# Two banks in turn for the sums of y and for delta, and a convolution in six steps whose relu term TensorE adds in the bank

## The chip, the cores and the metric

The kernel runs on one core of a Trainium2 chip. The metric is the time of one execution on the device, in microseconds. TensorE (PE) does the matmuls, VectorE (DVE) and GpSimd (POOL) the elementwise work, ScalarE (ACT) the activations and copies, and SyncE (SP) issues the DMAs. Each engine works through its own queue in order and waits at an instruction until what it needs is there. A matmul writes to a bank of PSUM, of 512 fp32 numbers for each of 128 partitions.

## The reference

The model has an input of 4 images of 64 x 64 positions with 96 channels and two layers. The first is a convolution and a selective scan over 192 inner channels with 16 states each, in four directions; the second is attention with a feed-forward part. What matters here is in the first:

```python
def selective_scan(u, delta, A, Bs, Cs, D, delta_bias):
    ...
    delta = jax.nn.softplus(delta + delta_bias[None, :, :, None])
    def step(h, inp):
        ut, dt, Bt, Ct = inp
        dA = jnp.exp(dt[..., None] * A[None])
        h = dA * h + (dt * ut)[..., None] * Bt[:, :, None, :]
        y = jnp.einsum('bkdn,bkn->bkd', h, Ct)
        return (h, y)
...
xz = bilinear(x, W_in, s_in, b_in)
xp, z = jnp.split(xz, 2, axis=-1)
xc = xp.transpose(0, 3, 1, 2)
t = bq_quad(xc + move0_b[None, :, None, None])
...
t = jax.lax.conv_general_dilated(t, Wb, (1, 1), [(1, 1), (1, 1)], dimension_numbers=('NCHW', 'OIHW', 'NCHW'))
t = t + conv_b[None, :, None, None]
t = t + rp_b0[None, :, None, None]
t = jnp.where(t >= 0, t, prelu_a[None, :, None, None] * t)
t = t + rp_b1[None, :, None, None] + xc
xconv = jax.nn.silu(t)
...
out_y = selective_scan(xs, dts, A, Bs, Cs, Ds.reshape(K, Dn), dt_bias.reshape(K, Dn))
```

The prelu is a*t + (1 - a)*relu(t). The convolution's inputs and weights are signs, so the kernel holds them in fp8. `_gn(x)`, the group norm ahead of the layer, subtracts for each three channels their mean over an image, for which the kernel first forms sums over channels.

## The kernel before

**Pieces.** The scan is cut into 1536 pieces: 4 images x 4 directions (the order is in `KORD`) x 4 chunks of 1024 positions x 6 groups g of 32 channels x 4 quarters q of 4 states. A piece is a tile of 128 rows (32 channels x 4 states) by 1024 positions. `Scans.run` (L1323) goes through them one after the other. In step i it issues, in this order:

- loads for later pieces (`dl`: delta and delta times u; `bc`: B and C);
- the earlier directions' sums, once in four pieces (`load_sums`), and the copy of the last column of piece i-1's state for the next chunk (`carry`, ACT, L1271);
- if i mod 8 is 3: `evacuate(i - 4)`, in which ACT copies the sums of y out of PSUM (L1316) and four stores are noted;
- `decay(i + 1)`: ACT takes the exponential into a PSUM tile dA (L1231; there are two of these);
- `reduce(i - 3)`: PE sums over states with four matmuls (L1302) into the bank of y, and adds the earlier directions' sums at the end of a group (L1307). One bank holds two groups, that is eight pieces;
- `inject(i + 4)`: POOL multiplies delta times u by B, into a tile w (nine of these in turn, free again after `reduce`);
- a product h x C left to POOL by the step before, if any;
- `scan(i)`: DVE's scan, and then the product h x C on DVE, or left to POOL for the next step. Which one is decided when the program is built, from a tally of both engines' work (L1248 to L1258).

All DVE and POOL work beside the scan goes through one helper and has its line, L401. Stores are noted in `Later` and issued on SP at the end of that or a later step (L420).

**Lanes.** Beside the pieces, two kinds of generators are advanced by one stage in each step. Their stages lie between `yield`s. If i mod 8 is 0, a new `prepare` (L1130) is begun: it forms delta for a part of a chunk. Its stages are: eight matmuls into the bank dps (L1167); Abs and Relu on ACT (L1172, L1173); Exp and Ln, the latter into the bank (L1175, L1176); PE adds the relu part in the bank with an identity matmul (L1179); DVE multiplies by u (L1181); ACT copies delta out (L1185), and a store (`dld`) is noted, from which `dl` is loaded later. Three such prepares run ahead of the first piece. The other is the back lane, one generator after the other for the images: the prologue of image b + 2 (convolution among it) and the epilogue of image b (normalisation, attention, feed-forward).

**The convolution** (L567 to L635). An image has 16 parts: two halves of the channels by eight strips of 512 positions. A part has 18 taps, fp8 matmuls into one bank (L577), in four stages of 5, 4, 5 and 4, and a fifth stage in which ACT forms v and r = relu and PE forms xc in a second bank, pz. In the first four stages of the next part the part is finished: stage 0, two DVE additions into pz (L585 and L586: pz = S*pz + v, then pz = pz + (1 - a) r, `oma`); stage 1, Sign and Exp on ACT (L590, L598); stage 2, Ln and Exp (L600, L601); stage 3, u = pz * e on DVE (L604) and the copy of u by columns into `ut` (ACT, L614; POOL, L612, for image 0, whose prologue runs alone). Four parts fill one `ut`, which is then stored to `utd`; the rest of the prologue (`rw`) reads it to form the other directions, with `xr` on ACT (L659).

**csum** (L508 to L516): 32 matmuls with x as the weights and a column of ones, all added in one bank, then a copy (`cs`) and a matmul over groups of channels.

**PSUM.** dA takes two tiles of two banks. The other four banks are b0 and b1 for the back lane, y, and dps.

Of the kernel before, what the change touches and what calls it, by code (L numbers as in the profile page):

```python
# [53 lines left out]
def hybrid_kernel(ctx: ExitStack, tc: tile.TileContext, a: dict, out: bass.AP):  # L54
# [82 lines left out]
    acs, acb, oma = ctile("acs", [96, 2]), ctile("acb", [96, 2]), ctile("oma", [96, 2])  # L137

# [18 lines left out]
    def weights():  # L157
# [28 lines left out]
        def transposed(dst, srcs):  # L186

            count[0] += 1
            ps = p.ps.tile([128, 1024], BF16, name=f"tps{count[0]}", tag=("y", "dps")[count[0] % 2])
# [87 lines left out]
        nc.vector.tensor_scalar(oma, pv[:, :, PRELU], -1.0, 1.0, ALU.mult, ALU.add)  # L277
        yield
# [72 lines left out]
        ps = p.ps.tile([128, 512], F32, name="tpd", tag="dps")  # L351
# [125 lines left out]
def prologue(c, b, xts=None):  # L477
# [11 lines left out]
    with tc.tile_pool(name=f"xg_{b}", bufs=1) as xgp:  # L489
# [3 lines left out]
        with tc.tile_pool(name=f"cv_{b}", bufs=1) as cvp:  # L493
# [14 lines left out]
            csum = bank("csum", 0)[0:96, 0:1]  # L508
            for i in range(NT):
                nc.tensor.matmul(csum, xts[i // 8][:, i % 8, :], c.ones1, start=(i == 0), stop=(i == NT - 1))  # L510
                if i % 8 == 7:
                    yield
            cs = f32("cs")[0:96, 0:1]
            nc.scalar.copy(cs, csum)
            gsum = bank("gsum", 1)[0:96, 0:1]
# [48 lines left out]
            prev = None  # L564
            two = c.p.dA.tile([128, CH], F32, name=f"cv2_{b}", tag="dA") if alone else None
            utp = sub.enter_context(tc.tile_pool(name=f"ut_{b}", bufs=1))
            for n, part in enumerate(parts + [None]):  # L567
# [5 lines left out]
                for s in range(4):  # L573
                    if part:
                        for j, t in taps[(0, 5, 9, 14)[s] : (5, 9, 14, 18)[s]]:
# [5 lines left out]
                            )  # L581
                    if prev:
                        ph, pq, pz, v, r, pn = prev
                        if s == 0:
                            c.vec.scalar_tensor_tensor(pz, pz, pv[:, ph, S_X : S_X + 1], v, ALU.mult, ALU.add)  # L585
                            c.vec.scalar_tensor_tensor(pz, r, c.oma[:, one(ph)], pz, ALU.mult, ALU.add)  # L586
                        elif s == 1:

                            sg = f32("sg" + pn)[0:96, 0:128]
                            nc.scalar.activation(  # L590
                                sg.bitcast(F8).rearrange("p (h e i) -> p h e i", h=8, e=2),
                                pz.rearrange("p (h i e) -> p h e i", h=8, e=2), AF.Sign, saturate=False,
                            )
                            for m in range(3):
                                g0 = 64 * (m // 2) + 32 * ph
                                c.later.store(xgw[g0 : g0 + 32, m % 2, 128 * pq : 128 * pq + 128], sg[m::3, :])
                            e = f32("e" + pn)[0:96]
                            nc.scalar.activation(e, pz, AF.Exp, scale=-1.0)  # L598
                        elif s == 2:
                            nc.scalar.activation(e, e, AF.Ln, bias=1.0)  # L600
                            nc.scalar.activation(e, e, AF.Exp, scale=-1.0)  # L601
                        else:
# [3 lines left out]

                            if pq % 4 == 0:
                                ut = utp.tile([96, IW, 32], F32, name=f"ut{pn}_{b}", tag="ut")
                            at = 8 * (pq % 4)
                            dst, src = ut[:, :, at : at + 8], u.rearrange("p (h w) -> p w h", w=IW)  # L610
                            if alone:
                                nc.gpsimd.tensor_copy(dst, src)  # L612
                            else:
                                nc.scalar.copy(dst, src)  # L614
                            if pq % 4 == 3:
                                rows = slice(8 * pq - 24, 8 * pq + 8)
                                c.later.store(
                                    c.utd[b][ph].rearrange("p (w h) -> p w h", h=IH)[:, :, rows], ut, after=1
                                )
                    yield  # L620
                if part:
# [9 lines left out]
                    )  # L631
                    prev = (h, q, pz, v, r, nm)
                    yield
            c.later.flush()
            sub.close()  # L635


# [459 lines left out]
class Scans:  # L1097
# [225 lines left out]
    def run(self, back):  # L1323
# [20 lines left out]
        for m in (1, 2):  # L1344
            self.load_dl(m)
# [113 lines left out]
```

## Time and profile before

| what | value |
|---|---|
| median of 3 runs (lowest to highest) | 5541.44 us (5539.87 to 5541.87) |
| the profiled execution | 5540.64 us |
| its span, first to last instruction | 5538.9 us |
| mean granted clock of TensorE | 0.714 |
| first scan to end of the last scan | 269.0 to 5421.4 us |

The page gives the span in 40 equal slices of 138 us. Each digit is the busy share of a slice in tenths, and PEclk is the granted clock of TensorE, in tenths:

```profile
PE   6456665576557766577656766544676564444677
...
DVE  3299999999999999899999999999999999999984
ACT  4467776777666667677766666755556775555554
POOL 2199999999999999899999999999999999999981
PEclk8667776678767876667777777766787766566778
```

After two slices of prologue and before the last, DVE and POOL are busy for 90% or more almost throughout, while PE and ACT go up and down with the stage of the back lane. By the number of the piece, the back lane has the convolution of image 1 from 69 to 149, that of image 2 from 264 to 344 and that of image 3 from 647 to 727; epilogues and the other prologue stages fill most of the rest, and for 264 pieces (1000 to 1093, 1290 to 1355, 1372 to 1475) it waits, with nothing to do beside the scan.

### The profile page before, as it was taken

Reading aid. Unit: us, or ns where it says so; the run is one execution under the profiler, and the core shown is the slowest. Engines: PE = TensorE matmul, PEld = TensorE weight load, DVE = VectorE, ACT = ScalarE, POOL = GpSimd, SP = SyncE. Lnnn points to the kernel's source line nnn. Section 1 sums busy time; section 2 is a strip of 40 time slices with the busy share of each in tenths; the row PEclk is TensorE's granted clock in tenths of the full one; section 3 lists DMA queues with packets and bytes.
Section 4 is the critical chain, followed back from the end, with each engine's and each line's share of the span. In section 5 each row is a group of like instructions: output and inputs, shape, how many; then the busy total and the mean of one; then the engine's idle time right before and its main releaser. Section 6 shows DMA issues by size and latency. Waiting matters only on the chain. (4 is left out here: it accounts for less than half of the span.)

```text
span 5538.9 us, 62371 instructions
## 1 busy us (share of the span) xinstructions
PE 3432.7 (62%) x20197; PEld 1356.7 (24%) x20197; DVE 5052.4 (91%) x3237; ACT 3556.7 (64%) x5564; POOL 4994.2 (90%) x2262
## 2 busy tenths in 40 slices
PE   6456665576557766577656766544676564444677
PEld 3222222222223222222222222211232121111223
DVE  3299999999999999899999999999999999999984
ACT  4467776777666667677766666755556775555554
POOL 2199999999999999899999999999999999999981
PEclk8667776678767876667777777766787766566778
DMA  4456666866766566666656566665666665665652
GB/s 78 118 179 198 207 194 193 258 193 199 220 203 194 194 205 199 218 217 207 205 193 212 185 200 210 212 211 191 210 215 186 191 205 198 205 208 190 207 159 60
DMA packets 613244, 1069.93 MB, mean 193 GB/s; under 512 B 225083, under 2 KB 343924, under 8 KB 611124
## 3 DMA queue, kind: packets, MB, share of 16 engines
q1 hardware_dynamic: 599428, 1065.88, 61.4%
q8 instruction: 159, 2.61, 0.2%
q10 hardware_dynamic: 13488, 0.07, 0.1%
q14 instruction: 169, 1.38, 0.1%
HBM read 833.20 MB, written 229.38 MB: 192 GB/s over the span
## 5 line engine op out<-in xcount | busy, mean ns | idle before, releaser
L401 POOL TENSOR_TENSOR w<-dl,bc 128x1024 f32<-128x1024 f32 x1536 | 3579.9, 2356 | 166.7 <-PE yp L1302 93.2
L1231 ACT ACTIVATE dA<-dl,anm 128x1024 f32<-128x1024 f32 x1536 | 1715.6, 1117 | 477.0 <-DVE w L401 291.5
L1302 PE MATMUL yp<-w,sum 128*32 128x256 f32 x12288 | 1261.6, 507 | 1083.2 <-ACT ys L1316 621.9
L401 DVE TENSOR_TENSOR_SCAN dA<-dA,cy,w 128x1024 f32<-128x1024 f32 x706 | 1654.4, 2343 | 94.7 <-ACT dA L1231 83.4
L401 POOL TENSOR_TENSOR w<-h,bc 128x1024 f32<-128x1024 f32 x596 | 1402.6, 2353 | 93.7 <-DVE h L401 85.2
L401 DVE TENSOR_TENSOR w<-dA,bc 128x1024 f32<-128x1024 f32 x940 | 1151.4, 1225 | 47.7 <-DVE dA L401 0.5
L401 DVE TENSOR_TENSOR_SCAN h<-dA,cy,w 128x1024 f32<-128x1024 f32 x446 | 1043.3, 2340 | 9.2 <-ACT dA L1231 8.7
L1302 PEld LDWEIGHTS yp<-w,sum 128*32 128x32 f32 x12288 | 308.0, 127 | 2136.9 <-issue 705.4
L1271 ACT COPY cy<-dA 128x1 f32<-128x1 f32 x707 | 110.8, 157 | 692.0 <-DVE w L401 690.7
L401 DVE TENSOR_TENSOR_SCAN dA<-dA,w 128x1024 f32<-128x1024 f32 x234 | 534.2, 2283 | 22.3 <-ACT dA L1231 18.0
L577 PE MATMUL cv<-tp,cw 96*96 96x512 fp8e5 x1152 | 359.9, 456 | 85.6 <-ACT r L627 70.5
L401 DVE TENSOR_TENSOR_SCAN h<-dA,w 128x1024 f32<-128x1024 f32 x150 | 341.8, 2279 | 24.4 <-POOL w L401 23.6
L1179 PE MATMUL dps<-sp,ident 128*128 128x512 f32 x378 | 356.8, 1043 | 0.0
L1307 PE MATMUL yp<-ya,back 128*128 128x256 f32 x576 | 237.8, 534 | 0.0
L577 PEld LDWEIGHTS <-cw 96*96 96x96 fp8e5 x1152 | 159.0, 146 | 277.5 <-issue 223.8
L1271 ACT COPY cy<-h 128x1 f32<-128x1 f32 x445 | 82.7, 186 | 145.6 <-DVE h L401 144.5
L847 PE MATMUL yc<-eys,mean 96*96 96x512 f32 x240 | 134.6, 713 | 33.3 <-DMA eys<-yd 14.5
L1307 PEld LDWEIGHTS yp<-ya,back 128*128 128x128 f32 x576 | 123.9, 248 | 127.8 <-issue 97.1
L1172 ACT ACTIVATE pd<-dps,dbias,pvd 128x512 f32<-128x512 f32 x189 | 143.8, 761 | 16.4 <-PE dps L1167 13.0
L1173 ACT ACTIVATE sp<-dps,dbias,pvd 128x512 f32<-128x512 f32 x189 | 144.7, 766 | 0.0
L401 DVE TENSOR_TENSOR pd<-dps,pu 128x512 f32<-128x512 f32 x189 | 127.6, 675 | 4.6 <-DMA dl<-dld 4.3
L1316 ACT COPY ys<-yp 128x512 f32<-128x512 f32 x192 | 111.7, 582 | 30.2 <-PE yp L1307 24.3
(282 smaller groups left out, 4017.6 us busy)
## 6 DMA issues: line engine op xcount, KB each, us to landing
dl<-dld SPq DMA_DIRECT2D x768, 512.0 KB
bc<-bcd SPq DMA_DIRECT2D x512, 512.0 KB
dld<-pd SPq DMA_DIRECT2D x126, 512.0 KB
yd<-ys SPq DMA_DIRECT2D x768, 64.0 KB
dld<-pd SPq DMA_DIRECT2D x126, 256.0 KB
ya<-yd SPq DMA_DIRECT2D x192, 128.0 KB
pu<-ud SPq DMA_DIRECT2D x32, 512.0 KB
pu<-utd SPq DMA_DIRECT2D x31, 512.0 KB
```

The source lines that it names most:

```text
L401: return getattr(self.eng, name)(out, *args, **kw)
L577: nc.tensor.matmul(ps, c.cw[:, j, t, 96 * h : 96 * h + 96], tpad[j][:, 8 * q + dy : 8 * q + dy + 8, dx : dx + IW], start=(j == 0 and t == ...
L847: self.c.nc.tensor.matmul(ps, w, x, start=(i == 0), stop=(i == len(pairs) - 1))
L1172: nc.scalar.activation(d[:, 0], ps, AF.Abs, scale=sc, bias=bi)
L1173: nc.scalar.activation(t, ps, AF.Relu, scale=sc, bias=bi)
L1179: nc.tensor.matmul(ps, c.ident, t, start=False, stop=True, skip_group_check=True)
L1231: c.nc.scalar.activation(t, self.dlt[i // NQ][0], AF.Exp, scale=c.anm[:, g, NQ * KORD[e] + q : NQ * KORD[e] + q + 1])
L1271: self.c.nc.scalar.copy(self.carries[g, q], h[:, CH - 1 : CH])
L1302: c.nc.tensor.matmul(y[32 * x : 32 * x + 32, g % 2, :], c.sum4, prod[:, 256 * x : 256 * x + 256], start=(q == 0), stop=(q == NQ - 1 and no ...
L1307: c.nc.tensor.matmul(y[:, g % 2, :], w, src, start=False, stop=(n == len(more) - 1))
L1316: c.nc.scalar.copy(t, y[:, :, ::-1] if k >= 2 else y)
```

## The change

Six edits, which go through the same functions:

1. **Banks.** The separate bank dps is gone. The sums of y alternate between two banks, y0 and y1, by eights of pieces. A prepare forms delta in the one that the sums do not use at that moment (`bank()`). Two set-up transposes take y0 and y1 as well.
2. **Order.** `evacuate` is issued after `decay(i + 1)`, no longer ahead of it.
3. **Prepares.** They begin at i mod 8 = 3, and have one more `yield` between Ln and the identity matmul. A fourth one runs ahead of the first piece, after the first three loads of `dl`; for that one more tile of the pool w is used at the start.
4. **Convolution** of images 1 to 3. Taps come four to a stage, in five stages, and with that of v and r there are six. The second addition on DVE is replaced by a matmul into pz with a diagonal matrix of 1 - a (`omad`, made once by two POOL instructions), in a stage of its own; Sign and Exp, Ln and Exp, and u follow one stage later each. The copy by columns is put off to stage 0 of the part that follows, and for the last part to just ahead of the final flush of stores.
5. **csum.** Eight matmuls with the ones as weights give a row of 4 x 96 sums; ACT copies the row, and four small matmuls turn and add it into a column, with one more `yield`.
6. **Carries.** One tile of four columns per group for four tiles of one column.

```diff
@@ prologue, csum
-            csum = bank("csum", 0)[0:96, 0:1]
-            for i in range(NT):
-                nc.tensor.matmul(csum, xts[i // 8][:, i % 8, :], c.ones1, start=(i == 0), stop=(i == NT - 1))
-                if i % 8 == 7:
+            csum = bank("csum", 0)[0:1, 0 : 4 * DM]
+            for i in range(0, NT, 4):
+                nc.tensor.matmul(
+                    csum, c.ones1, xts[i // 8][:, i % 8 : i % 8 + 4, :].rearrange("p i e -> p (i e)"),
+                    start=(i == 0), stop=(i == NT - 4),
+                )
+                if i % 8 == 4:
                     yield
+            row = f32("csr")[0:1, 0 : 4 * DM]
+            nc.scalar.copy(row, csum)
+            ps = bank("cst", 1)[0:96, 0:1]
+            for i in range(4):
+                nc.tensor.matmul(
+                    ps, row[:, DM * i : DM * i + DM], c.ones1[0:1, :], start=(i == 0), stop=(i == 3)
+                )
+            yield
             cs = f32("cs")[0:96, 0:1]
-            nc.scalar.copy(cs, csum)
-            gsum = bank("gsum", 1)[0:96, 0:1]
+            nc.scalar.copy(cs, ps)
+            gsum = bank("gsum", 0)[0:96, 0:1]
@@ prologue, convolution
-                for s in range(4):
+                for s in range(4 if alone else 5):
                     if part:
-                        for j, t in taps[(0, 5, 9, 14)[s] : (5, 9, 14, 18)[s]]:
+                        per = 5 if alone else 4
+                        for j, t in taps[per * s : min(18, per * s + per)]:
...
+                    if s == 0 and turned:
+                        by_columns(*turned)
+                        turned = None
                     if prev:
                         ph, pq, pz, v, r, pn = prev
                         if s == 0:
                             c.vec.scalar_tensor_tensor(pz, pz, pv[:, ph, S_X : S_X + 1], v, ALU.mult, ALU.add)
-                            c.vec.scalar_tensor_tensor(pz, r, c.oma[:, one(ph)], pz, ALU.mult, ALU.add)
+                            if alone:
+                                c.vec.scalar_tensor_tensor(pz, r, c.oma[:, one(ph)], pz, ALU.mult, ALU.add)
+                        elif s == 1 and not alone:
+                            nc.tensor.matmul(pz, c.omad[:, ph], r, start=False, stop=True, skip_group_check=True)
...
+            if turned:
+                by_columns(*turned)
             c.later.flush()
@@ Scans
+    def bank(self):
+        return max(0, self.at - 3) // 8 % 2
@@ prepare
-        ps = spare[3] if spare else p.ps.tile([128, 512], F32, name=f"dps_{nm}", tag="dps")
+        ps = spare[3] if spare else p.ps.tile([128, 512], F32, name=f"dps_{nm}", tag=f"y{1 - self.bank()}")
...
         nc.scalar.activation(ps, d[:, 0], AF.Ln, bias=1.0)
+        yield
         yield
@@ scan
-            self.carries[g, q] = c.p.cy.tile([128, 1], F32, name=f"cy_{i}", tag=f"cy{g}{q}")
+            if q == 0:
+                self.cys[g] = c.p.cy.tile([128, NQ], F32, name=f"cy_{i}", tag=f"cy{g}")
+            self.carries[g, q] = self.cys[g][:, q : q + 1]
@@ reduce
-            self.ydone[i // 8] = c.p.ps.tile([128, 2, 256], F32, name=f"yp_{i}", tag="y")
+            self.ydone[i // 8] = c.p.ps.tile([128, 2, 256], F32, name=f"yp_{i}", tag=f"y{i // 8 % 2}")
@@ run
-        w = [c.p.w.tile([128, CH], F32, name=f"w_s{x}", tag="w") for x in range(7)]
+        w = [c.p.w.tile([128, CH], F32, name=f"w_s{x}", tag="w") for x in range(8)]
...
+        u = c.p.pu.tile([128, CH], F32, name="pu_s", tag="pu")
+        for _ in self.prepare((w[7].rearrange("p (t l) -> p t l", t=2), w[4][:, 512:CH], u, ps[1][:, 512:CH])):
+            pass
...
+            if i + 1 < n:
+                self.decay(i + 1)
             if i % 8 == 3 and i > 8:
                 self.evacuate(i - 4)
-            if i + 1 < n:
-                self.decay(i + 1)
...
-            if i % 8 == 0 and self.todo:
+            if i % 8 == 3 and self.todo:
```

## The prediction

> **What bounds the kernel now.** I read the shares of busy time first, then the groups of instructions, then the waits, and at last busy time by stretches, since shares are means over stages.
>
> ```profile
> PE 3432.7 (62%) x20197; PEld 1356.7 (24%) x20197; DVE 5052.4 (91%) x3237; ACT 3556.7 (64%) x5564; POOL 4994.2 (90%) x2262
> ...
> L401 POOL TENSOR_TENSOR w<-dl,bc 128x1024 f32<-128x1024 f32 x1536 | 3579.9, 2356 | 166.7 <-PE yp L1302 93.2
> ...
> L1302 PE MATMUL yp<-w,sum 128*32 128x256 f32 x12288 | 1261.6, 507 | 1083.2 <-ACT ys L1316 621.9
> ...
> L401 POOL TENSOR_TENSOR w<-h,bc 128x1024 f32<-128x1024 f32 x596 | 1402.6, 2353 | 93.7 <-DVE h L401 85.2
> L401 DVE TENSOR_TENSOR w<-dA,bc 128x1024 f32<-128x1024 f32 x940 | 1151.4, 1225 | 47.7 <-DVE dA L401 0.5
> ```
>
> DVE and POOL are the bound together. Each of the 1536 pieces costs a scan on DVE (2.28 to 2.34 us) and the product with B on POOL (2.356 us); the product with C falls to either (1.225 us on DVE, 2.353 us on POOL), and the tally in `scan` shares it out until both are level. Between first and last scan (269.0 to 5421.4 us, 1536 pieces, 3.355 us each) the trace sums to 229 us of idle DVE and 205 of idle POOL. So there are two things to win: work (whatever leaves DVE is shared by both) and that idle time.
>
> The waits tempt to look elsewhere:
>
> ```profile
> PE yp L1302 <- ACT ys L1316: 621.9, 141, 10.8
> ...
> DVE dA L401 <- ACT dA L1231: 101.3, 86, 5.5
> ...
> POOL w L401 <- PE yp L1302: 93.6, 58, 8.6
> ...
> ACT ut L614 <- DVE u L401: 91.6, 45, 3.6
> ```
>
> Columns: total, times, longest. PE loses 622 us because the one bank y must be copied out (L1316) before the next eight pieces may be summed. The stretches decide whether that matters; the first below is image 2's convolution, the others have no prologue or epilogue beside the scans:
>
> ```profile
> core 0: us, PE busy (x) PEld busy (x) DVE busy (x) ACT busy (x) POOL busy (x), PEclk, DMA share, GB/s
> 1161.00:1441.00 280.00, 186.11 (x1091) 73.63 (x1089) 272.82 (x182) 201.28 (x309) 275.14 (x119) 0.78 0.69 204
> ...
> 3645.00:3943.00 298.00, 146.39 (x914) 51.00 (x914) 293.59 (x169) 156.59 (x237) 294.55 (x130) 0.62 0.61 197
> 4598.00:4807.00 209.00, 96.94 (x634) 32.09 (x634) 206.21 (x118) 110.61 (x162) 205.59 (x90) 0.60 0.60 195
> ```
>
> From 3645 to 3943 PE waits 69 us for ys, by far its most, yet DVE is 98.5% and POOL 98.8% busy. That wait is off the path: products lie in nine w buffers, and PE may be some two pieces (6.7 us) late before POOL lacks one. During the convolution the bound engines are 97.4% and 98.3% busy; it costs by its work, not by stalls.
>
> **What the Trainium skill says.** "Perfetto Trace Analysis", Identifying Performance Opportunities, says that a consistent bubble can mean that SBUF or PSUM ran out for the next tile, on the engine that should be saturated. PE's wait for ys is such a bubble, but on an engine at 62%, and the stretches show it to be free. "PSUM — Partial Sum Buffer", The four PSUM rules, says that a matmul without the first flag adds where the bank has been written; L1179 does so with relu already, and the new relu matmul of the convolution takes the same way (that no value is lost there I assume). "TensorE: Matmul & The Clock Gate", What's actually happening, says that an idle PE falls back to half clock. The trace agrees: a pair of L1179 matmuls takes 2.08 us at 284 us and about 1.1 elsewhere, granted clock 0.60 to 0.82 by stretch. I price PE work at both.
>
> **Work that leaves.** In the convolutions of images 1 to 3 the second DVE addition goes (image 0 keeps it):
>
> ```profile
> L401 DVE SCALAR_TENSOR_TENSOR cz<-cz,pv,v x64: 730/746/756, 91.3 to 2715.0; 96x512 f32<-96x512 f32 x64
> L401 DVE SCALAR_TENSOR_TENSOR cz<-r,oma,cz x64: 750/751/753, 92.2 to 2715.8; 96x512 f32<-96x512 f32 x64
> ```
>
> 48 x 0.751 = 36.0 us less on DVE. The order of instructions in the changed kernel has 587 products with C on POOL and 949 on DVE, for 596 and 940. So DVE: -36.0 + 9 x 1.225 = -25.0 us; POOL: 9 x 2.353 = -21.2 us. The lesser counts: **-21**. It is spread over stages where both are over 97% busy, so little of it can fall into idle time.
>
> In its place come 48 fp32 matmuls 96x512 on PE. The nearest rows (the epilogue's xc, 976 ns, and L1179, 1043) give 1 to 2.1 us, 48 to 100 us in all. PE is 66% busy in this stage. The matmul stands one step after the DVE addition that it waits for; queued behind it on PE are the next taps and the sums of the next piece. DVE reaches the addition at the end of piece i; then PE catches up on one piece, of two that it may be late. Both ends: 0, or 0.5 us x 48 = +24 if the two pieces run out. I take **0**. If the cover goes, POOL's wait for yp shows it.
>
> **The order of ACT.** The copy of ys moves behind decay(i+1). Idle DVE ahead of scan k, by k mod 8, sums in the trace to 31.2 us at 4, which is where the copy stands ahead of the decay, and to 13.5 on the mean of the other seven. So 17.7 us can go; but some of it is DVE work of the lanes at that place. I take half, **-9** (0 to -18).
>
> **Two banks.** yp(8m+8) now goes into the other bank and no longer waits for ys. But the delta sums (dps) of the prepare begun in the same step use the bank just copied, and their eight matmuls (285 ns each) now wait for ys, one decay (1.117 us) later than before. On PE the wait only moves; queued behind it are the reduces of the next pieces, as before. On PSUM release: the lane now ends at step 8m+9 with the copy of delta, and yp next needs that bank at 8m+11, two steps of slack. From the stretches I take **0**; ends: -20 (POOL's 93.6 us for yp, 29 of it in turns and conv-free prologue stages, partly gone) and +40 (the slower rival).
>
> **Prepares.** They begin at i mod 8 = 3 for 0, with one more step, so the store of delta is issued about four pieces earlier for its reader, since one more prepare is made before the first scan: 14 pieces ahead of piece 24c where it was 10, and 9 are needed. SP waited for it: the queue's wait for dld<-pd is 172.6 us in 58 times, but of DVE and POOL hardly any; **0** (0 to -5). The fourth prepare stands on DVE's queue ahead of the first scan, and its u (512 KB) comes behind three dl loads. In the timeline scans 0 and 1 run from 269.0 to 273.6, then DVE waits 9.2 us for POOL till 282.8. So up to some 9 us are covered. The extra step of the four prepares costs about a microsecond: **+1** (0 to +6, if u lands after about 278 us).
>
> **Convolution in six steps, and the turned copy.** Taps per step fall from 5 to 4; same work, 16 more steps per image. The lane is some 11 pieces late after each convolution, and the later lanes wait anyway: by the order of instructions everything from image 2's epilogue on stands at the same piece. ut (L614) goes to the next part's first step, which takes away ACT's 91.6 us for u: ACT has slack, 0. But the last of each image is now copied directly ahead of its store, and the following xr (L659) waited already 4.6, 4.6 and 4.7 us for that transfer (utd<-ut). One step less of cover is up to 3 us on an in-order ACT, ahead of a decay with about 1 to 2 us of slack: +2 x 3, some hidden: **+4** (0 to +8).
>
> **csum.** 32 matmuls 96x1 (297 ns, plus weight loads of 280) become 8 of 1x384, a row copy and four tiny matmuls: PE work is about equal, and one round trip PE-ACT-PE (one step) is added, twice inside the scans with effect. The stage loses 8.6 us there now on ACT's wait for csum. **+2** (-3 to +4). The carry tile changes no instruction on DVE; ACT's 692 us of idle time cover it: 0.
>
> **Sum.** -21 - 9 + 0 + 0 + 1 + 4 + 2 = -23, against the profiled execution's 5540.6 us (span 5538.9 and 1.7 around it; the median of the runs is 5541.4, 0.8 more): 5517.6, so 5518. This case's own range, from the ends that may lie together, is 5500 to 5530.
>
> **Rivals.** (1) The work leaves but in-order queues give it back: the copy's order gives 0, xr +8, csum +4, start +6. Time 5540.6 - 21 + 18 = 5538. For it: every stage with lanes idles 2 to 12% already, from just such round trips. Against: in the convolution itself they idle under 3%.
> (2) The banks were on the path after all: half of POOL's 86 us for yp (in 330 to 5360) goes as well. 5540.6 - 21 - 43 = 5477. For it: that wait stands first for POOL; against: its releaser is PE, and PE is late in those places because of epilogue matmuls (PE 73 to 79% busy), not of ys, which costs PE only 3 to 16 us there.
> (3) Slower: PE at the delta sums. They wait for ys behind a decay that itself waits for DVE, so PE stands still until DVE has finished the piece before, every eighth piece, and then has to catch up. Where PE is over 66% busy (about half of the 189 prepares) it doesn't, and POOL lacks w. At 0.6 us each, 95 x 0.6 = 57: 5540.6 - 23 + 57 = 5575. It decides from the point where PE is more than two pieces behind. For it: POOL waits for yp in those stages already. Against: 141 waits of 4.4 us on the mean were free so far, and the new one replaces them.
>
> **How the numbers follow.** Forecast 0.52, rival 1 0.17, rival 2 0.10, rival 3 0.21. What a measurement of this kernel can tell from no change is about 0.2%, 11 us: 5530 to 5552. The forecast's case and rival 2 give 0.62, of which 0.02 end within the bound; rival 1 lies within it but for 0.01, which goes slower with rival 3: 0.60, 0.18, 0.22. The range leaves out half of rival 2 below (0.05) and two thirds of rival 3 above (0.14): 5478 to 5560.
>
> **What would show it.** Right: cz<-r,oma,cz has 16 instructions, POOL's w<-h about 587; PE's wait for ys moves from yp to dps and stays in the hundreds; DVE's idle time ahead of k mod 8 = 4 falls to that of its neighbours; stretches without lanes keep 3.17 to 3.18 us per piece. Wrong: POOL's wait for yp well over 94 us (rival 3) or under 50 (rival 2), or the pieces without lanes getting faster.

## The result, and the profile after

The changed kernel takes 5530.6 us (median of 4 runs, 5528.8 to 5534.1) against 5540.7 for the kernel before (5537.7 to 5541.9): a ratio of 0.9983, with a 95% interval of 0.9966 to 1.0001. That is some 10 us less, of 23 forecast, and the interval just takes in 1. The profiled execution took 5528.8 us, its span 5527.0.

First the shares of busy time and the groups of instructions from the page of the changed kernel (lines of the code have moved: L401 is L404, L1302 is L1340, L1316 is L1354, L1231 is L1267, L1167 is L1202).

```profile
PE 3478.7 (63%) x20133; PEld 1371.3 (25%) x20133; DVE 5025.5 (91%) x3198; ACT 3568.5 (65%) x5568; POOL 4975.1 (90%) x2255
...
L404 POOL TENSOR_TENSOR w<-dl,bc 128x1024 f32<-128x1024 f32 x1536 | 3578.8, 2356 | 158.7 <-PE yp L1340 69.6
...
L1340 PE MATMUL yp<-w,sum 128*32 128x256 f32 x12288 | 1289.5, 515 | 401.5 <-POOL w L404 260.0
L404 POOL TENSOR_TENSOR w<-h,bc 128x1024 f32<-128x1024 f32 x587 | 1381.1, 2353 | 114.4 <-DVE h L404 104.2
L404 DVE TENSOR_TENSOR w<-dA,bc 128x1024 f32<-128x1024 f32 x949 | 1162.4, 1225 | 48.7 <-issue 0.9
...
L1202 PE MATMUL dps<-gT,wdz 128*128 128x64 fp8e5 x1000 | 113.7, 313 | 339.4 <-ACT ys L1354 310.1
```

The work left as forecast: over the whole span DVE is busy 26.9 us less, POOL 19.1, and 587 products are on POOL. PE's wait for ys has gone from yp; it stands at the delta matmuls. The waits of the changed kernel show what of it is left (total, times, longest):

```profile
PE dps L1202 <- ACT ys L1354: 512.1, 135, 6.4
...
DVE dA L404 <- ACT dA L1267: 115.8, 87, 6.2
...
POOL w L404 <- DVE h L404: 104.2, 107, 4.3
...
POOL w L404 <- PE yp L1340: 71.5, 49, 6.8
```

DVE waits more for ACT's decays (115.8 us for 101.3), POOL more for DVE (104.2 for 85.2) and less for PE (71.5 for 93.6): idle time took the place of work. From the third scan to the end of the last, DVE works 27.0 us less, but idles 237.3 us for 217.4. By stretches, image 2's convolution first and then two stretches without a back lane:

```profile
1188.00:1525.00 337.00, 240.11 (x1362) 94.55 (x1361) 327.61 (x206) 236.48 (x362) 329.51 (x144) 0.79 0.68 206
4585.00:4793.00 208.00, 100.26 (x640) 34.10 (x643) 205.45 (x118) 109.58 (x159) 205.00 (x90) 0.58 0.59 192
4848.00:5179.00 331.00, 167.12 (x1034) 59.42 (x1033) 324.80 (x186) 172.96 (x265) 325.57 (x143) 0.62 0.62 198
```

The columns are PE, PEld, DVE, ACT and POOL. DVE and POOL are level to within 5 us in each, and 97 to 99% busy. Without a lane a piece still takes 3.15 to 3.18 us.

To place the loss I sum from the traces, for each stage of the back lane, its time less 3.176 us for each of its pieces (the rate of the stretches without a lane). "Start" runs from the first scan; rw is the re-ordering after a convolution. In the traces the convolutions of the kernel before lie at the pieces 63 to 147, 258 to 342 and 641 to 725, some six earlier than the places given ahead of the prediction (so the stretch from 1161 us that stands there for image 2's begins 20 us late); in the changed kernel they lie at 65 to 166, 278 to 379 and 679 to 780. Where the stages are cut a piece earlier or later, a row can differ by up to 5 us.

| stage | before | changed | difference |
|---|---|---|---|
| start, to the first convolution in the scans | 10.5 | 6.3 | -4.2 |
| three convolutions | 65.6 | 44.6 | -21.0 |
| three rw | 20.0 | 32.7 | +12.7 |
| csum and the stages round it, images 2 and 3 | 29.6 | 20.2 | -9.4 |
| epilogues of images 0 and 1 | 71.0 | 71.1 | +0.1 |
| epilogue of image 2 | 34.6 | 41.3 | +6.7 |
| the rest, to the last scan | 42.7 | 43.1 | +0.4 |
| sum | 274.0 | 259.3 | -14.7 |

The convolutions gain what was forecast, but the stall of edit 4's late copy falls just behind the cut, into rw; the two rows together gain 8.3 us. The gain at the start isn't one: the first scan now waits for the fourth prepare, while the third runs when it did (below). From the third scan to the end of the last the kernels take 5138.7 and 5131.5 us, 7.2 less; this stretch I use to compare, and call it T. Each T is from one profiled execution. Where code and order are the same two traces give the same: image 1's convolution takes 332.4 us with the changed kernel and with three of its variants below. It isn't so everywhere: the last 61 pieces, with the same instructions in the same order on DVE, ACT and POOL, take 232.8 us in conv_csum and 238.0 in conv_csum_prompt. A difference in T of some 6 us or less is therefore no verdict by itself, and the ratio of the runs has to say the same.

### The profile page after: what moved, and what is told of

The parts are those of the page before. It is cut to its first block, busy times and chain, and to the rows that moved or that the text cites. A ratio compares the mean times of both kernels' runs of the same rounds, so it can differ in the third digit from the quotient of the medians.

```text
span 5527.0 us, 62184 instructions
## 1 busy us (share of the span) xinstructions
PE 3478.7 (63%) x20133; PEld 1371.3 (25%) x20133; DVE 5025.5 (91%) x3198; ACT 3568.5 (65%) x5568; POOL 4975.1 (90%) x2255
## 5 line engine op out<-in xcount | busy, mean ns | idle before, releaser
L404 POOL TENSOR_TENSOR w<-dl,bc 128x1024 f32<-128x1024 f32 x1536 | 3578.8, 2356 | 158.7 <-PE yp L1340 69.6
L1267 ACT ACTIVATE dA<-dl,anm 128x1024 f32<-128x1024 f32 x1536 | 1714.6, 1116 | 495.5 <-DVE w L404 282.7
L404 DVE TENSOR_TENSOR_SCAN dA<-dA,cy,w 128x1024 f32<-128x1024 f32 x711 | 1665.8, 2343 | 98.7 <-ACT dA L1267 94.1
L1340 PE MATMUL yp<-w,sum 128*32 128x256 f32 x12288 | 1289.5, 515 | 401.5 <-POOL w L404 260.0
L404 POOL TENSOR_TENSOR w<-h,bc 128x1024 f32<-128x1024 f32 x587 | 1381.1, 2353 | 114.4 <-DVE h L404 104.2
L404 DVE TENSOR_TENSOR w<-dA,bc 128x1024 f32<-128x1024 f32 x949 | 1162.4, 1225 | 48.7 <-issue 0.9
L404 DVE TENSOR_TENSOR_SCAN h<-dA,cy,w 128x1024 f32<-128x1024 f32 x441 | 1031.6, 2340 | 8.6 <-ACT dA L1267 8.5
L1340 PEld LDWEIGHTS yp<-w,sum 128*32 128x32 f32 x12288 | 316.3, 129 | 1487.4 <-issue 710.4
L404 DVE TENSOR_TENSOR_SCAN dA<-dA,w 128x1024 f32<-128x1024 f32 x238 | 543.3, 2283 | 29.1 <-ACT dA L1267 21.6
L404 DVE TENSOR_TENSOR_SCAN h<-dA,w 128x1024 f32<-128x1024 f32 x146 | 332.5, 2278 | 10.5 <-ACT dA L1267 9.1
L1202 PE MATMUL dps<-gT,wdz 128*128 128x64 fp8e5 x1000 | 113.7, 313 | 339.4 <-ACT ys L1354 310.1
L1215 PE MATMUL dps<-sp,ident 128*128 128x512 f32 x376 | 279.7, 834 | 47.0 <-ACT dps L1211 46.7
L1202 PEld LDWEIGHTS <-wdz 128*128 128x128 fp8e5 x1024 | 95.1, 152 | 427.3 <-issue 395.1
L1202 PE MATMUL dps<-gT,wdy 128*128 128x64 fp8e5 x504 | 59.3, 320 | 204.1 <-ACT ys L1354 202.0
L1207 ACT ACTIVATE pd<-dps,dbias,pvd 128x512 f32<-128x512 f32 x188 | 143.2, 761 | 22.6 <-PE dps L1202 22.6
```

The costliest lines, as they stand in the source:

```text
L404: return getattr(self.eng, name)(out, *args, **kw)
L1202: nc.tensor.matmul(pv[:, s], wd[:, k, s], gT[:, :, c0 : c0 + 16], start=(s == 0), stop=(s == 7))
L1207: nc.scalar.activation(d[:, 0], ps, AF.Abs, scale=sc, bias=bi)
L1215: nc.tensor.matmul(ps, c.ident, t, start=False, stop=True, skip_group_check=True)
L1267: c.nc.scalar.activation(t, self.dlt[i // NQ][0], AF.Exp, scale=c.anm[:, g, NQ * KORD[e] + q : NQ * KORD[e] + q + 1])
L1340: c.nc.tensor.matmul(y[32 * x : 32 * x + 32, g % 2, :], c.sum4, prod[:, 256 * x : 256 * x + 256], start=(q == 0), stop=(q == NQ - 1 and no ...
```

## The experiments

Theory 1: the convolution brings its 21 us, and the prepares' place, the banks and ACT's order give part back. Theory 2: the convolution gives half back itself. All ratios are to the kernel before, with their 95% intervals.

| kernel | ratio | first scan to end, us | T, us |
|---|---|---|---|
| before | 1 | 5152.5 | 5138.7 |
| changed | 0.9983 (0.9966 to 1.0001) | 5137.5 | 5131.5 |
| conv_alone | 1.0004 (0.9996 to 1.0012) | 5152.1 | 5138.3 |
| conv_undone | 1.0039 (1.0027 to 1.0052) | 5164.0 | 5158.5 |
| evac_alone | 1.0003 (0.9995 to 1.0011) | 5153.4 | 5139.6 |
| evac_first | 0.9966 (0.9953 to 0.9978) | 5133.0 | 5126.5 |
| prep_place | 1.0027 (1.0017 to 1.0038) | 5158.7 | 5152.0 |
| start_4 | 0.9957 (0.9944 to 0.9971) | 5125.3 | 5118.6 |
| start_4_evac_first | 0.9979 (0.9973 to 0.9986) | 5136.9 | 5130.9 |
| start_4_short | 0.9964 (0.9952 to 0.9977) | 5123.8 | 5117.5 |
| turn_prompt | 0.9982 (0.9974 to 0.9990) | 5131.5 | 5125.8 |
| start_4_prompt | 0.9960 (0.9948 to 0.9972) | 5118.2 | 5112.7 |
| rw_later | 0.9955 (0.9942 to 0.9967) | 5122.4 | 5115.7 |
| conv_shift | 1.0000 (0.9992 to 1.0008) | 5141.1 | 5135.0 |
| csum_old | 1.0004 (0.9995 to 1.0012) | 5143.9 | 5137.6 |
| csum_alone | 1.0012 (1.0005 to 1.0018) | 5150.6 | 5136.8 |
| omad_five | 1.0019 (1.0012 to 1.0026) | 5162.2 | 5148.4 |
| conv_csum | 0.9962 (0.9948 to 0.9977) | 5132.2 | 5118.4 |
| conv_prep | 0.9987 (0.9981 to 0.9994) | 5140.2 | 5134.3 |
| conv_csum_prompt | 0.9951 (0.9937 to 0.9964) | 5130.8 | 5117.0 |

### The convolution, alone and undone

`conv_alone` is the kernel before with edit 4 (and 6, for room); `conv_undone` is the changed kernel without edit 4.

> The kernel before with the new convolution alone (six steps, relu term by TensorE, late turned copy; the carry tile goes with it for its room). Theory 1 (the convolution brings what it should, the new place of the prepares gives part back): DVE and POOL lose 21 to 25 us of work, xr after the convolution costs 2 to 4, so 5519 to 5524, faster than the changed kernel by 7 to 12. Theory 2 (the convolution itself gives half of it back): 5528 to 5533, as the changed kernel.

> The changed kernel with the convolution of before. Theory 1: the banks, the order of ACT, the prepares and csum cost 7 to 12 us, 5547 to 5553, with DVE idle ahead of the scans k mod 8 = 6 and 7 in place of 0 to 4. Theory 2: they cost nothing, 5538 to 5543.

Neither theory had this. Alone the convolution moves nothing; the other edits alone cost 20 us of T; together they gain. So part of the others lets its gain through, and another part costs.

From the third scan on, DVE works 26.7 us less in conv_alone than before and idles 26.4 us more. Its convolutions take 57.8 us above the lane-free rate for 65.6, so they keep 8 of the 21 us: DVE idles 37.2 us in them for 16.7, and POOL waits 14.2 us for yp for 1.9, which is the sign that the forecast named for PE's cover running out (in the convolutions of the changed kernel this wait is 0). The epilogues of images 0 and 1, in which no instruction differs, lose 9 us (79.7 for 71.0).

### csum, the partner

`csum_alone` is the kernel before with edit 5, `conv_csum` that with edits 4, 5 and 6, `csum_old` the changed kernel with the old csum and one empty stage behind it:

```diff
             nc.scalar.mul(negm, gsum, -1.0 / (3 * L))
+            yield
```

> The changed kernel with the csum of before and one empty stage behind it, so that all later stages stand at the same pieces. Theory A (32 matmuls with weight loads keep ACT waiting in cs, in front of a decay): ACT waits 4 to 10 us for csum again, scans 5143 to 5149 us for 5137.5. Theory B, as the prediction had it: 5135 to 5137, the saved round trip.

> The kernel before with the new convolution (alone: scans 5152.1) and the new csum. If csum with its 10.0 and 9.5 us of ACT waiting ate part of what the convolution brought: 5140 to 5147. If not: 5149 to 5154.

> The kernel before with the new csum and no other edit. If csum is worth by itself what it added to the new convolution (19.9 us), the scans take 5131 to 5137 us for 5152.5. If the two are partners, because in the old convolution's place csum made ACT wait 8.6 and 4.2 us and not 10.0 and 9.5: 5142 to 5150.

csum_old loses 6.1 us of T, and 0.21% by the runs (theory A). With the new convolution the new csum is worth 19.9 us, far more than expected, on the old one 1.9 of T (its runs even show 0.12% more): the two don't add. The timeline of conv_alone shows what the old csum does (start, length, instruction, in brackets the idle time before it and its releaser):

```profile
1089.20 2.69 PE L513 MATMUL csum<-ones,xt 128*96 128x1 f32 x16 [5.91 <-DMA xt<-in_x]
...
1101.06 2.72 PE L513 MATMUL csum<-ones,xt 128*96 128x1 f32 x16
...
1103.82 0.15 ACT L517 COPY cs<-csum 96x1 f32<-96x1 f32 x1 [9.99 <-PE csum L513]
...
1103.92 1.12 ACT L1254 ACTIVATE dA<-dl,anm 128x1024 f32<-128x1024 f32 x1
...
1105.15 2.36 DVE L404 TENSOR_TENSOR_SCAN dA<-dA,cy,w 128x1024 f32<-128x1024 f32 x1 [6.88 <-ACT dA L1254]
```

The image has landed late. Four blocks of 2.7 us and the sums of the pieces between them stand in PE's queue; ACT has come to the copy of the result and waits 9.99 us with a decay behind it, and DVE idles 6.9. In the changed kernel a csum matmul takes 486 ns for 384 columns, with a load of 84, where 298 and 280 were needed for one column; these durations overlap, but PE has 16 of them in place of 64, and for image 2 they keep it busy for 7.2 us in place of 10.7:

```profile
L514 PEld LDWEIGHTS csum<-xt,ones x64: 79/84/126, 31.7 to 2441.0; 128*1 128x1 f32 x64
L514 PE MATMUL csum<-xt,ones x64: 483/486/844, 31.7 to 2441.3; 128*1 128x384 f32 x64
```

ACT's waits there are 1.8 and 0.7 us (images 2 and 3) in the changed kernel, 8.6 and 4.2 before, 10.0 and 9.5 in conv_alone. The stages round csum and the first stages of the next image explain 15 us of conv_csum's gain over conv_alone (34.0 us above the lane-free rate to 18.9), the epilogues of images 0 and 1 another 13 (79.7 to 66.8), where no instruction differs: the lane stands otherwise against the prepares there. Other stages gave some 8 back. In csum_alone the stages round csum gain some 7 us as well, and these epilogues lose some 8. So what makes partners of the two edits lies for the greater part in stages that neither changes.

### The work without the stages

`omad_five` is the kernel before, where only the addition moves to TensorE:

```diff
                         if s == 0:
                             c.vec.scalar_tensor_tensor(pz, pz, pv[:, ph, S_X : S_X + 1], v, ALU.mult, ALU.add)
-                            c.vec.scalar_tensor_tensor(pz, r, c.oma[:, one(ph)], pz, ALU.mult, ALU.add)
                         elif s == 1:
+                            nc.tensor.matmul(pz, c.omad[:, ph], r, start=False, stop=True, skip_group_check=True)
```

> The kernel before with its five-stage convolution, where only the second addition of DVE is replaced by the matmul, in the stage of Sign and Exp; stages and places stay as they were. If the work that leaves DVE is worth its 21 us wherever it leaves, the scans take 5129 to 5136 us for 5152.5. If ACT, which now waits for PE ahead of Sign, hands the gain back as DVE's wait for a decay: 5141 to 5153.

It loses 9.7 us: the waits show why.

```profile
ACT sg L596 <- PE cz L593: 105.3, 48, 5.5
```

48 times ACT stands 2.2 us on the mean at Sign for the new matmul, which is behind PE's sums. In the convolutions DVE's wait for a decay rises from 3.9 to 34.4 us, so with 24 us less work on DVE the kernel is slower. In conv_alone, where the matmul has a stage of its own, ACT waits for it only twice, 2.2 us in all, and the loss is gone, though nothing is gained.

### The order of ACT, and the prepares' place

`evac_alone` is the kernel before with edit 2, `evac_first` the changed kernel without it, `prep_place` the kernel before with edit 3 (own bank for delta). `start_4` is the changed kernel with

```diff
-            if i % 8 == 3 and self.todo:
+            if i % 8 == 4 and self.todo:
```

`start_4_evac_first` is that without edit 2, `start_4_short` that without the added `yield`.

> The kernel before with the copy of the y sums behind the decay, and no other edit. By the prediction: 9 us less, 5532, idle DVE ahead of k mod 8 = 4 down from 31 us to about 14. Rival: PE waits 1.1 us longer for the one bank of y, and what DVE gains at 4 it loses a piece later: 5538 to 5543.

> The changed kernel with the copy of the y sums ahead of the decay again. By the prediction the copy's new place is worth 9 us: 5540. Theory 1: its idle time comes back only in part, since the stall then stands at the prepare's activations, and delta's matmuls get their bank 1.1 us sooner: 5528 to 5535. With the old place DVE idles again ahead of k mod 8 = 4.

> The kernel before with prepares begun at 3, one more stage between Ln and the matmul, and a fourth prepare ahead of the scans; delta has its own bank and y its one. If the place of the prepares costs in itself, the scans take 5158 to 5166 us for 5152.5, as with the changed kernel under the old convolution (5164.0). If the shared banks cost, 5149 to 5155.

> The changed kernel with prepares begun at i mod 8 = 4 for 3, one step after the copy of y that they share the bank with. Theory A (the eight delta matmuls stand on PE behind the wait for ys, and with them Abs and Relu on ACT ahead of a decay): PE's wait dps for ys falls from 512 us to under 150, and the scans take 5127 to 5133 us, as with the copy ahead of the decay (5133.0). Theory B (it is the place of the prepare's ACT work, not the wait): 5134 to 5143, the idle time of DVE moves from k mod 8 = 6 to 7.

> Prepares begun at 4 and the copy of y ahead of the decay again. If the copy's late place cost only by the delta matmuls behind it, nothing is left to gain: scans 5122 to 5129 for 5125.3. If its place is worth the forecast's 9 us where nothing else is in the way: 5131 to 5137.

> Prepares begun at 4 without the added stage between Ln and the matmul, so that delta leaves its bank a piece earlier. PE's wait yp for the copy of delta (328 us) falls below 150. If that wait is on the path the scans take 5115 to 5121; if it is off it, 5123 to 5130, or more where the matmul now waits for Ln.

The copy's late place gains 12.3 us of T if prepares begin at 4 (start_4 against start_4_evac_first), nothing if they begin at 0 (evac_alone), and loses 5.0 if they begin at 3 (the changed kernel against evac_first). Beginning at 3 costs 13.3 in the kernel before (prep_place), and beginning at 4 wins 12.9 over the changed kernel. The runs agree with each of these: start_4 against start_4_evac_first 0.22% less, the changed kernel against evac_first 0.17% more (with overlapping intervals, and 5.0 lies within the scatter of T, so this loss is likely, not certain), prep_place 0.27% over the kernel before, start_4 0.26% under the changed kernel. The waits of start_4:

```profile
PE yp L1340 <- ACT pd L1221: 328.2, 100, 7.2
...
PE dps L1202 <- ACT ys L1354: 110.4, 79, 4.0
...
DVE dA L404 <- ACT dA L1267: 98.5, 71, 10.1
```

PE's wait dps for ys falls from 512 to 110 us as theory A had it, and DVE's wait for decays by 17. But the link that I drew between them is not there: Abs and Relu wait for the delta matmuls as long as before (ACT pd for PE dps is 22.6 us in the changed kernel, 24.2 in start_4). Nor does prep_place, where delta waits for no copy of y, escape the cost. And start_4_short only moves the new wait, 328 us of yp for the copy of delta: it falls to 76, the identity matmul waits 257 us for Ln instead, and T stays within 1.1 us:

```profile
PE dps L1214 <- ACT dps L1211: 256.8, 96, 7.4
```

So none of these waits of PE is seen to cost.

What is left is the place of the prepare's activations. Idle DVE ahead of the scans, by k mod 8, summed from the traces (gaps over 0.15 us, from the fourth scan on):

| kernel | 0 | 1 | 2 | 3 | 4 | 5 | 6 | 7 |
|---|---|---|---|---|---|---|---|---|
| before | 21.9 | 23.1 | 4.3 | 18.5 | 31.2 | 7.2 | 10.5 | 8.7 |
| evac_alone | 16.6 | 22.4 | 4.1 | 17.9 | 16.0 | 2.0 | 21.7 | 6.9 |
| changed | 20.6 | 6.1 | 12.7 | 8.2 | 8.4 | 14.4 | 47.6 | 25.2 |
| evac_first | 19.8 | 6.1 | 11.7 | 8.2 | 19.7 | 10.7 | 44.9 | 19.0 |
| prep_place | 22.5 | 9.0 | 10.9 | 4.3 | 12.1 | 12.4 | 39.2 | 18.6 |
| start_4 | 30.2 | 15.8 | 8.0 | 6.3 | 9.4 | 14.1 | 15.5 | 22.6 |
| start_4_evac_first | 34.4 | 16.9 | 6.8 | 6.4 | 18.6 | 11.5 | 19.3 | 21.9 |

Abs and Relu come ahead of the decay of scan 3, 6 or 7 as the prepare begins at 0, 3 or 4, Exp and Ln ahead of the next. So at 4 two things stood ahead of the decay in the kernel before: the copy of y, and Exp and Ln of a prepare. Either alone takes the stall there from 31.2 us to 16.0 (evac_alone, the copy moved) or 12.1 (prep_place, the prepares moved), both together to 8.4.

In evac_alone the idle time ahead of the scans falls by 17.8 us in all, as much as the forecast allowed, and as much comes back ahead of DVE's work for the lanes: 61.2 us for 42.9, of which 12.1 at the prepare's product with u, which waits mostly for PE (11.9 us of 16.7). PE in turn waits longer for the copy than the 622 us of before, as the rival had it:

```profile
PE yp L1302 <- ACT ys L1316: 775.2, 152, 11.3
```

The idle time follows the prepare's activations, and a good part of it lies behind a piece whose product is POOL's: DVE then needs only 2.3 us, in which ACT has to do the carry, Abs and Relu (1.5 us) and the decay. With a start at 3 such a piece stands ahead of that decay 83 times of 188 (74 in prep_place), with one at 0 or 4 only 65 and 59 times (before, start_4). DVE's idle time behind those pieces is 29.8 us of 47.6 in the changed kernel, 21.0 of 39.2 in prep_place, 14.1 of 18.5 before and 9.5 of 22.6 in start_4.

It also needs the back lane. In prep_place 33.5 of the 39.2 us at 6 stand where ACT has work of the back lane ahead of the same decay too (104 of the 192 places). In the stretches without a back lane, where prepares run all the same, there is no such gap ahead of any scan, and those 253 pieces take 799.1 us for 799.4 before: there the place of the prepares costs nothing. The epilogue of image 2 stands at the same piece in every kernel; above the lane-free rate it takes 33 to 37 us where prepares begin at 0, 36 to 43 at 3 and 31 to 38 at 4.

That agrees with the loss in direction, but it is not the whole of it. Of the 13.2 us by which DVE idles longer in prep_place only 3.7 stand ahead of scans (129.0 us for 125.3, over all k); 9.2 stand ahead of work for the lanes, 8.0 of them at the prepare's product with u (12.6 for 4.6):

```profile
DVE pd L401 <- PE dps L1180: 12.6, 7, 6.2
```

How these come from the prepares' place no run shows.

### The late copy by columns

`turn_prompt` makes the last part of each convolution copy its u in its own stage; `start_4_prompt` and `conv_csum_prompt` do so in start_4 and conv_csum:

```diff
-                            if alone:
+                            if alone or not part:
                                 by_columns(*turned)
                                 turned = None
```

`rw_later` is start_4 with three empty stages behind the flush:

```diff
             c.later.flush()
+            if not alone:
+                for _ in range(3):
+                    yield
```

> The changed kernel, but the last part of each convolution copies its u by columns in its own stage, one stage ahead of the flush of stores; the number of stages is the same. Theory A (the late copy leaves xr waiting 8 to 9 us for the transfer, three times, and most of that reaches DVE): xr waits 4.7 us each, and the stages from the end of the convolutions to the end of the re-ordering lose 6 to 12 us in all; scans 5126 to 5132 us for 5137.5, the time 0.1 to 0.2% under the changed kernel. Theory B (ACT's wait is covered): the wait falls, scans 5135 to 5140.

> The changed kernel with prepares begun at i mod 8 = 4 (scans 5125.3 us) and, in images 1 to 3, three empty stages of the back lane between the flush of stores and the re-ordering that follows. Theory A (ACT's 25 us of waiting for the ut transfer, ahead of decays, reaches DVE): ACT no longer waits for it in these images, the stages from the end of a convolution to the end of the re-ordering lose 8 to 15 us in all, scans 5111 to 5118. Theory B (where the lane stands against the prepares matters as much): the wait goes and the scans take 5119 to 5131.

> The changed kernel with prepares begun at 4 (scans 5125.3) and the last part of each convolution copied by columns in its own stage (which took 6.0 us off the changed kernel's scans). If the two add: 5116 to 5122 and a time of 0.5% under the kernel before. If the stall only moves, as with the empty stages: 5123 to 5129.

> The kernel before with the new convolution, the new csum (scans 5132.2) and the last part of each convolution copied by columns in its own stage. xr then waits 4 to 7 us a time for 7 to 8.5; if that counts as in the changed kernel, 5124 to 5130 us.

The timeline of the changed kernel at the end of image 1's convolution:

```profile
813.15 1.08 ACT L590 COPY ut<-u 96x512 f32<-96x512 f32 x1
...
815.42 0.63 SPq L423 DMA_DIRECT2D utd<-ut  x1
...
825.02 0.59 ACT L690 CAST xr<-xa 128x512 bf16<-128x512 f32 x1 [8.87 <-DMA utd<-ut]
...
826.82 2.36 DVE L404 TENSOR_TENSOR_SCAN dA<-dA,cy,w 128x1024 f32<-128x1024 f32 x1 [6.17 <-ACT dA L1267]
```

From the issue of the store to xr it is 9.6 us; ACT waits 8.9 of them with a decay behind, and DVE idles 6.2. Before it was 4.7:

```profile
776.97 0.58 ACT L659 CAST xr<-xa 128x512 bf16<-128x512 f32 x1 [4.67 <-DMA utd<-ut]
```

Copied in its own stage (turn_prompt), the waits were 8.2, 7.5 and 4.0 us for 8.9, 8.0 and 8.1, and T fell by 5.7; 5.9 in start_4, but only 1.4 in conv_csum. These are within the scatter of T. By the runs the ratio is 0.9982 for 0.9983, 0.9960 for 0.9957 and 0.9951 for 0.9962: nothing in the first two, and 0.11% with overlapping intervals in the third. So the waits are shorter, and a gain in time is not shown. With three empty stages these waits go but for 1.1 and 3.2 us, the rw stages gain 8.7 us, the stages round csum and the free ones lose as much, and the time is that of start_4 (0.9955 for 0.9957), as theory B had it.

### One stage's shift

`conv_shift` is the changed kernel with one empty stage ahead of each convolution:

```diff
+            if not alone:
+                yield
             parts = [(h, q) for h in range(2) for q in range(NQ8)]
```

> The changed kernel with one empty stage ahead of the convolution of images 1 to 3, which puts six-stage parts one piece later against prepares that come each eight pieces. Theory A (six and eight have a common factor, so the same activations meet in every third part or never): the convolutions' idle DVE, 24 us in all, changes by 8 us or more either way. Theory B (it evens out): it stays within 4 us, and so do the scans with 5137.5.

The convolutions' idle DVE is 27.9 us for 24.0, T 3.5 longer, the time 0.17% more. An empty stage, without any work, goes with differences of this size, so they are no verdict on an edit.

### Convolution and prepares without the new csum

`conv_prep` is the kernel before with edits 3, 4 and 6.

> The kernel before with the new convolution and the new place of the prepares, which keep their own bank (the latter alone: scans 5158.7). If the six-stage convolution needs the prepares at 3 for its gain, 5130 to 5138. If both are worth what they are alone, 5156 to 5161.

The scans, 5140.2, lie just above the first case, and T is 17.7 under prep_place's. Its csum waits are 11.3 and 12.7 us, so here most of the convolution's gain comes through an old csum as well. What hides it in conv_alone therefore also hangs on where the lane stands against the prepares, and isn't settled by csum alone.

## Why the prediction was wrong

- **Work that leaves, -21: right as work, and as time only here.** The numbers of products are exact, and the convolutions lose 21.0 us above the lane-free rate. PE's matmul takes 0.59 us a pass, 1.1 a pair, and costs no measured wait of POOL in its stage. With the same work gone the convolutions keep only 8 us of this in conv_alone, where POOL does wait for yp, 12 in start_4 and 13 in conv_csum. That just the forecast's 21 come out here is in part luck.
- **Prepares, 0: the step that failed.** I priced their new begin only by SP's stores and the start. Their ACT work also moves, to ahead of other decays, where it meets the back lane's and more often follows a short DVE piece. Begin at 3: 13.3 us in the kernel before; put to 4, 12.9 come back. How this cost comes about is traced only in part (above).
- **Two banks, 0: not contradicted.** "On PE the wait only moves" was right as said: 512 us of it stayed. In start_4 400 of these go and 261 come back at yp. No run changes the banks alone; evac_first and conv_prep differ by them and by csum, 7.8 us of T, of which csum_old puts 6.1 on csum.
- **The place of the back lane, 0: too simple.** The lane is 18, 36 and 54 pieces later after the three convolutions, not some 11, and that was priced at nothing because later stages wait. But stages in which no instruction differs change with where they stand against the prepares: 9 us for the epilogues of images 0 and 1 in conv_alone.
- **The order of ACT, -9: wrong in this kernel.** The forecast put the 31.2 us ahead of k mod 8 = 4 down to the copy and overlooked Exp and Ln, which stood there too. Alone the copy's new place gives back all that it takes away. Next to a prepare that begins at 3, where the copy stands one step ahead of Abs on ACT, the stall at 4 falls by 11 us, those at 5 to 7 grow by 13, and the edit costs 5.0 of T; beside one that begins at 4 it gains 12.3.
- **xr, +4: too small as a wait.** The waits grew by 11 us in three places. Shorter ones take 5.7 off T, but no clear time off the runs.
- **csum, +2: wrong sign.** I took PE's work to be equal, where it fell from 10.7 to 8 us (7.2 and the four small matmuls), and overlooked that ACT stands in front of a decay while PE works off the blocks. In the changed kernel it is worth -6.1, and behind the new convolution alone -19.9.
- **Start, +1: about right.** The timeline shows the fourth prepare ahead of the first scan, and the cover that the forecast named:

```profile
259.37 13.83 POOL L404 TENSOR_TENSOR w<-dl,bc 128x1024 f32<-128x1024 f32 x6 [60.19 <-DMA dl<-dld]
267.17 0.69 DVE L404 TENSOR_TENSOR w_s<-dA_s,pu_s 128x512 f32<-128x512 f32 x1 [20.45 <-DMA pu_s<-utd]
...
269.60 4.47 DVE L404 TENSOR_TENSOR_SCAN h<-dA,w 128x1024 f32<-128x1024 f32 x2 [1.74 <-ACT dA L1267]
```

  DVE waits for u and scans 10.2 us after POOL's first product, 2.4 before; the third scan comes 16.1 and 16.2 us after it.
- **The sum.** The edits don't add. From the chain before, conv_csum (-20.3), changed (-7.2), the remaining edits 1, 2 and 3 cost 13.1 us of T, as much as prep_place alone; that the two agree so well is chance, since the order's 5 us lie in the first. Rival 3 was at the right edit, with a loss of some 13 us for its 57, but not on the path that it named: POOL's wait for yp fell from 93.6 to 71.5. Rival 1 named two of the places where the gain went, xr and the in-order queues.

Of all versions conv_csum_prompt, at 0.9951, is the only one whose interval lies below that of the changed kernel; those of rw_later (0.9955) and start_4 (0.9957) just meet it. The three aren't told apart from each other; the first needs none of edits 1, 2 and 3.

## What to carry to other kernels

When two engines share the bound and a third feeds them just in time, price a moved step by what it puts ahead of the feeding instruction, and at which pieces, not by its wait totals: here 400 us of PE's wait for one copy went, 261 us came up behind another, and the wait of ACT behind them stayed as it was. A gain in work must be traced to the next in-order wait, which can hand it back in a stage where no instruction has changed. Before two edits are judged, try each alone and both together.

## What I had not expected of the hardware

- A column of sums by TensorE was cheaper here with the data moving and the ones standing: 16 fp32 passes of 384 columns (486 ns each, a load of 84) kept PE busy for 7.2 us, where 64 passes of one column (298 ns, a load of 280) took 10.7. The four small matmuls that turn the row take 0.8 us more.
- 48 matmuls put one stage too close behind DVE made ACT wait 105 us, and T grew by 9.7 us, though DVE had 24 us less to do.
